# A pipelined Mamba stage kernel: starting each stage's side work 19 units sooner, and loading its inputs part by part

## The chip, the cores and the metric

The kernel runs on one core of one Trainium2 chip. The metric is device time in microseconds (us) for the whole program; lower is better. A core has five engines that matter here, each with its own queue of instructions which it works off in order: TensorE (PE, matrix products, whose weight loads the profile lists as PEld), VectorE (DVE), ScalarE (ACT), GpSimd (POOL) and SyncE (SP), which in this kernel only issues DMA transfers. Sixteen DMA engines move the data of all transfers.

## The reference

Four layers, each `x = x + layer(group_norm(x))`, work on four images of 96 channels and 64 x 64 pixels in float32.

- Layer 0: an attention over super-pixels, with a 5 x 5 depthwise convolution beside it.
- Layer 1 ("l1"): a projection to 192 channels, a 3 x 3 convolution, then a selective scan along four ways through the image (rows forward, rows backward, columns forward, columns backward), whose four outputs are summed, normalised over the channels, gated, and put through a small convolution net.
- Layer 2: a 3 x 3 convolution.
- Layer 3 ("l3"): convolutions, again a selective scan along four ways, the sum, a normalisation, a gate and a channel mixing.

The scan is the heavy part. For 192 channels, 16 states and 4096 steps it computes `h = h * exp(delta * A) + delta * u * B`, then `y = sum over states of h * C`. The sum of the four ways needs the two row ways and, turned by a transpose of the image, the two column ways:

```python
y = oy[:, 0] + inv[:, 0] + why + invwhy
```

Layers 1 and 3 have one scan for each of the four images, so there are eight scans.

## The kernel before

**Stages and units.** The eight scans run one after another in the order of `SCANS` (line 37): l1 of images 0 and 1, l3 of images 0 and 1, l1 of images 2 and 3, l3 of images 2 and 3. Each is a stage, numbered 0 to 7. A stage has 32 groups: four ways, four chunks of 1024 steps, two halves of 96 channels. A group has 12 units of 8 channels x 16 states = 128 rows. So a stage has `per` = 384 units, and the program 3072. What comes ahead of stage 0 (layers 0 and the input of layer 1 of image 0) and behind stage 7 runs alone.

**One unit.** `unit` (line 2160) writes out the instructions of one unit on all engines: SP fetches the decay rows of the unit four ahead (`fetch`, line 2065, 512 KB into one of twelve `rep` buffers; `AHEAD` = 4), ACT makes exponentials of those of the unit two ahead (`decays`, line 2073), DVE scans (`scan`, line 2093) and multiplies with B (line 2086), POOL multiplies with C (line 2105), PE spreads inputs (`drive`) and, each fourth unit, sums over states (`collect`). When a group ends, `output` (line 2125) puts its sum into `yo`, and at the start of the next unit SP stores it to `y_row` or `y_col` in DRAM and counts `stored[0]` up by one. Group g of the program counts as stored in unit 12 (g + 1) + 2.

**Side work.** Beside a stage runs the work of another image that is not the scan: `BESIDE` (line 38) names it. Beside stages 0, 3 and 4 it is `first` (layer 0 and the input of l1 of the next image), beside 1, 2, 5 and 6 `second` (the end of l1 for an image whose scan is done, layer 2 and the input of l3), beside 7 three times `third` (the end of l3 and of the program) and then `last`, which is `third` for the image that is being scanned. These are generators. Each `yield` ends a step and says what it is charged: nothing (None) for a step on PE, charged by its matmul time, a number in half microseconds for others, `WAIT` for the whole rest of the unit.

**The planner.** Each unit gets a budget of `PACE` of its stage, in us of PE time. The unit's own `drive` costs 0.43 of it and `collect`, each fourth unit, 1.71. The class `Slots` then takes steps in up to three places of the unit for as long as 0.3 or more is left; a debt is carried over. So PACE sets how densely the side work is strewn, and where in the stage it ends. In the main loop (line 2256 on) the work of a stage begins at its unit 0. At unit `per - NG - LEAD - 1` = 365 all that is left of it is written out at once (`work.run()`), since at 366 the first group of the next stage is prepared from what it made. From 365 to 383 nothing runs beside the scan.

**The sums' loads.** `second`, `third` begin with `directions` (line 1529). For each half h of the channels it waits until the scan's outputs are stored, then loads the row sum into V and the column sum into a tile `yc`, in chunks of 1024 columns. y_row and y_col hold 96 channels in four blocks of 24 rows with 8 rows of gap behind each, so `ungapped` (line 1118) issues four transfers of 24 rows for each chunk: 32 for each half, all from one slot, then a charge of 4. Then come 16 turns: ACT copies 512 columns of `yc` transposed (line 1546), PE adds the row part and the turned part, ACT copies the sum to V (line 1556). `last` and, for its late chunks, `finish` use `ungapped` too.

**Group norm beside the scan.** `group_norm_on_scalar` (line 1161) has 4 copies with a sum, 8 squares with a sum and 4 scalings on ACT, each charged 1. **Several generators at once.** `weave` (line 1307) goes round among up to `depth` generators, moving on after each step that has a number.

Of the kernel before, what the change touches and what calls it, by code (L numbers as in the profile page):

```python
# [9 lines left out]
F32 = mybir.dt.float32  # L10
# [7 lines left out]
B, C, H, W = 4, 96, 64, 64  # L18
# [9 lines left out]
CH = 1024  # L28
NCH = L // CH
# [7 lines left out]
SCANS = (("l1_", 0), ("l1_", 1), ("l3_", 0), ("l3_", 1), ("l1_", 2), ("l1_", 3), ("l3_", 2), ("l3_", 3))  # L37
# [1 line left out]
          (("first", 3),), (("second", 2),), (("second", 3),), (("third", 0), ("third", 1), ("third", 2), ("last", 3)))  # L39
GN_EPS = 1e-5  # L40
PHI_EPS = 1e-12
PACE = (2.95,3.45,3.45,2.95,2.95,3.45,3.45,3.2)


PHI_SAFE = 10.0
# [154 lines left out]
def _view(t, slot, rows=None):  # L200
    n, m, shape = slot
    v = t[: rows or t.shape[0], n : n + m]
    if len(shape) == 1:
        return v
    names = "abcd"[: len(shape)]
    return v.rearrange(f"p ({' '.join(names)}) -> p {' '.join(names)}",
                       **{k: s for k, s in zip(names, shape)})
# [693 lines left out]
def streams(ctx: ExitStack, tc: tile.TileContext, x, wts, cst, out, wat, cat, flag):  # L901
# [3 lines left out]
    nc = tc.nc  # L905
# [12 lines left out]
    cols = keep.tile([128, 5], F32, name="cols")  # L918
# [88 lines left out]
    def img(t):  # L1007
        return t.rearrange("p (a b) -> p a b", b=W)
# [8 lines left out]
    def mm(o, lhsT, rhs, first=True, last=True):  # L1017

        lhsT, rhs = lhsT[:], rhs[:]
        if lhsT.shape[0] == 96 and lhsT.tensor.name in padded and rhs.tensor.name in padded:  # L1020
            lhsT, rhs = full(lhsT), full(rhs)
        n = 1
        for d in rhs.shape[1:]:
            n *= d
        m = o.shape[0]
        passes = 1 if rhs.dtype == BF16 else 1.07 if m == 32 else 2 if m == R + 2 * N else 4
        spent[0] += n * passes / 2400
        nc.tensor.matmul(o, lhsT=lhsT, rhs=rhs, start=first, stop=last)  # L1028
# [4 lines left out]
    def bank():  # L1033
        if solo[0]:
            if not spare:
                t = ps.tile([128, CH], F32, tag="bx", name="bx")
                spare.extend((t[:, PCH:], t[:, :PCH]))
            return spare.pop()
        return ps.tile([128, PCH], F32, tag="one", name="one")
# [47 lines left out]
    with Stack(1) as T:  # L1087
        t0 = T.tile([128, cst.shape[1] - n2], F32, name="t0")
        nc.scalar.dma_start(out=t0, in_=cst[:, n2:])
        n, m, shape = wat["l1_alog"]  # L1090
# [4 lines left out]
        n, m, shape = cat["spread"]  # L1095
        nc.vector.tensor_copy(spread.rearrange("p a b -> p (a b)"), t0[:, n - n2 : n - n2 + m])
        for tag in ("l1_", "l3_"):
            decay[tag] = keep.tile([128, 4, E // 8], F32, name=tag + "decay")
            n, m, shape = cat[tag + "alogn"]
            src = _view(t0, (n - n2, m, shape))  # L1100
            if tag == "l3_":
                nc.scalar.activation(decay[tag], src, AF.Exp)
                src = decay[tag]
# [7 lines left out]
    def image(name, rows=96):  # L1111
        return [dram.tile([rows, L], F32, name=f"{name}{b}") for b in range(B)]
# [3 lines left out]
    y_row, y_col = ([image(f"{k}{h}_", 128) for h in range(2)] for k in ("yrow", "ycol"))  # L1116

    def ungapped(dst, src, cols):

        for q in range(4):  # L1120
            nc.sync.dma_start(out=dst[24 * q : 24 * q + 24], in_=src[32 * q : 32 * q + 24, cols])

    def group_norm(src, dst):

# [32 lines left out]
    def group_norm_on_scalar(src, dst):  # L1161

        st = small.tile([96, 8], F32, name="gs_st")
        for j in range(4):
            s = src[:, bass.ts(j, CH)]
            nc.scalar.activation(s, s, AF.Copy, accum_out=st[:, j : j + 1])
            yield 1
        mv = small.tile([96, 4], F32, name="gs_mv")
        nc.vector.tensor_reduce(mv[:, 0:1], st[:, 0:4], AX.X, ALU.add)
        yield 0.5  # L1170
        p = bank()
        mm(p[:96, 0:1], group[:96], mv[:, 0:1])
        yield
        nc.scalar.activation(mv[:, 1:2], p[:96, 0:1], AF.Copy, scale=-1.0 / L)
        yield 0.5
        for j in range(8):
            p = bank()
            nc.scalar.activation(p[:96], src[:, bass.ts(j, PCH)], AF.Square, bias=mv[:, 1:2], accum_out=st[:, j : j + 1])
            yield 1
        nc.vector.tensor_reduce(mv[:, 2:3], st, AX.X, ALU.add)  # L1180
        yield 0.5
        p = bank()
        mm(p[:96, 0:1], group[:96], mv[:, 2:3])
        yield
        nc.scalar.activation(mv[:, 2:3], p[:96, 0:1], AF.Sqrt, bias=eps[:96], scale=1.0 / L)
        yield 0.5
        nc.vector.reciprocal(mv[:, 2:3], mv[:, 2:3])
        nc.vector.tensor_mul(mv[:, 3:4], mv[:, 1:2], mv[:, 2:3])
        yield 0.5
        for j in range(4):  # L1190
            nc.scalar.activation(dst[:, 16 * j : 16 * j + 16, :], img(src)[:, 16 * j : 16 * j + 16, :], AF.Identity,
                                 scale=mv[:, 2:3], bias=mv[:, 3:4])
            yield 1

    def diagonals(pool, w, name="diag"):

# [110 lines left out]
    def weave(made, depth):  # L1307

        left, active = list(made), []
        while left or active:  # L1310
            if left and len(active) < depth:
                active.append(left.pop(0))
            for g in list(active):
                while True:
                    try:
                        v = next(g)
                    except StopIteration:
                        active.remove(g)
                        break
                    yield v  # L1320
                    if v is not None and not isinstance(v, tuple):
                        break

    def attention(b, xn, w, samp, dist):
# [204 lines left out]
    def directions(V, b, tag):  # L1529

        with Stack(1) as T:
            full = len(groups) // len(SCANS) * (SCANS.index((tag, b)) + 1)
            cols = []
            for h in range(2):
                while stored[0] < full - 1 + h:
                    yield WAIT
                t = T.tile([96, W, H], F32, name="yc", bufs=2)
                cols.append(t)
                for j in range(4):
                    ungapped(t.rearrange("p a b -> p (a b)")[:, bass.ts(j, CH)], y_col[h][b], bass.ts(j, CH))  # L1540
                    ungapped(V[:, h, bass.ts(j, CH)], y_row[h][b], bass.ts(j, CH))
                yield 4

            def turned(n):
                y = T.tile([96, PCH], F32, name="yt", bufs=2)
                nc.scalar.copy(img(y), cols[n // 8][:, :, 8 * (n % 8) : 8 * (n % 8) + 8].rearrange("p a b -> p b a"))  # L1546
                return y

            y = turned(0)
            for n in range(16):  # L1550
                v = V[:, n // 8, bass.ts(n % 8, PCH)]
                p = bank()
                mm(p[:96], ident[:96, :96], v, True, False)
                mm(p[:96], ident[:96, :96], y, False, True)
                yield
                nc.scalar.copy(v, p[:96])
                if n < 15:
                    y = turned(n + 1)
                yield 1

    def second(b):

# [362 lines left out]
    NG = 96 // 8  # L1925
    WAIT = "wait"
# [134 lines left out]
    def fetch(i):  # L2061

        g, m = place(i)
        rep = sp.tile([128, CH], F32, name="rep", bufs=12)
        nc.sync.dma_start(out=rep, in_=ready[g][1][8 * m : 8 * m + 8, :].unsqueeze(0).to_broadcast([N, 8, CH]))
        live[i] = [rep]
# [76 lines left out]
    AHEAD, BEHIND, LEAD = 4, 2, 6  # L2143
    DRIVE, SUM, SLOT = 0.43, 1.71, 0.5
    total = len(groups) * NG
    per = total // len(SCANS)
    store, waiting, stored, owed = [], [], [0], 0.0
# [5 lines left out]
    def catch_up(n):  # L2153
        for w in waiting:
            w[0] -= n
        for w in [w for w in waiting if w[0] <= 0]:
            waiting.remove(w)
            w[1]()
# [74 lines left out]
    def beside(s):  # L2233
        stages = {"first": first, "second": second, "third": third, "last": last}
        for n, b in BESIDE[s]:
            yield from stages[n](b)
# [3 lines left out]
    with tc.manual_schedule():  # L2240
        for _ in prepare(0):
            catch_up(9)
        catch_up(9)
        prep = Slots(prepare(1))
        for _ in range(LEAD):
            prep.begin(0)
            prep.end()
            catch_up(1)
        for i in range(AHEAD):
            fetch(i)  # L2250
        decays(0)
        decays(1)
        drive(0)
        drive(1)
        times_b(0)
        for i in range(total):
            s, at = divmod(i, per)
            g, m = divmod(i, NG)
            if at == 0:
                work, owed = Slots(beside(s)), 0.0  # L2260
            if m == NG - LEAD and g + 2 < len(groups):
                prep.run()
                prep = Slots(prepare(g + 2))

            if at == per - NG - LEAD - 1 and s < len(SCANS) - 1:
                work.run()

            owed = min(owed, 0.6) + PACE[s]
            owed = unit(i, prep, work, owed)
        for j in range(total - 4, total, 4):  # L2270
            collect(j)
            output(j)()
            stored[0] += 1
# [14 lines left out]
    p = bank()  # L2288
# [37 lines left out]
```

## Time and profile before

| What | us |
|---|---|
| median of 3 runs | 13741.8 |
| lowest and highest | 13741.55, 13748.16 |
| the profiled execution | 13771.14 |
| its span, first to last instruction | 13769.2 |
| ahead of the first scan | 648 |
| stage 0 | 1602 |
| stages 1 to 6, each | 1575 to 1581 |
| stage 7 | 1929 |
| behind the last scan | 122 |

Busy shares of the span: DVE 84%, PE 81% (matmuls are pipelined, so this isn't the share of its peak), POOL 75%, ACT 63%; mean granted clock of TensorE 0.901. The DMA engines were busy 76.2% of their time with SP's transfers.

Stage boundaries are the starts of the 1st, 385th, 769th, ... of the 3072 scan instructions (line 2093). Any unit's start is found in the same way, so a stretch of units of a stage is a stretch of time, and the busy times of all engines in it can be read. In stage 2 the last 19 units, with nothing beside the scan, take 73.1 us, or 3.85 each; the 143 units of side work in which PE has convolutions take 540.0, or 3.78 each.

### The profile page before, as it was taken

The page shows a single profiled execution, that of the slowest core. Times are in us where ns is not written, and L with a number is a line of the kernel's source. Part 1 is how long each engine was busy: PE and PEld are TensorE (multiplying, and loading weights), DVE is VectorE, ACT ScalarE, POOL GpSimd, SP SyncE. Part 2 cuts the span into 40 slices and gives each one's busy share as a digit, 9 for nine tenths or more (in the row PEclk, how much of TensorE's full clock was granted, in tenths as well). Part 3 has the DMA queues.
Part 4 walks back from the last instruction along what each step waited for, and adds up shares of the span by engine and source line. Part 5 has one row for each costly group of instructions (what it writes and reads, how often), then busy time and mean ns, then how long its engine had stood idle before and what let it go on. Part 6 is the DMA issues. An engine that isn't in the chain of part 4 may idle for free. (4 is left out here: it accounts for less than half of the span.)

```text
span 13769.2 us, 128385 instructions
## 1 busy us (share of the span) xinstructions
PE 11150.4 (81%) x40802; PEld 3349.2 (24%) x40802; DVE 11633.7 (84%) x7509; ACT 8718.5 (63%) x12338; POOL 10280.4 (75%) x4730
## 2 busy tenths in 40 slices
PE   9888886988779896888868887898969887777756
PEld 3322221322223221222212221232313222111111
DVE  1488998998889988889988898898889988887886
ACT  3366576667756676665766566667756676665654
POOL 1178887888878877788877888787878878666674
PEclk9899998999889897999989998998979998888867
DMA  0277788787878888778877788797888878777674
GB/s 11 68 172 197 200 224 215 201 218 203 224 195 223 210 210 212 188 194 214 232 190 198 195 216 227 192 228 198 213 214 204 224 201 229 185 196 188 172 195 115
DMA packets 840849, 2682.51 MB, mean 195 GB/s; under 512 B 111264, under 2 KB 113792, under 8 KB 840160
## 3 DMA queue, kind: packets, MB, share of 16 engines
q1 hardware_dynamic: 839504, 2672.34, 76.2%
q8 instruction: 324, 5.31, 0.2%
q14 instruction: 365, 2.99, 0.1%
q10 hardware_dynamic: 656, 1.87, 0.0%
HBM read 2179.90 MB, written 493.88 MB: 194 GB/s over the span
## 5 line engine op out<-in xcount | busy, mean ns | idle before, releaser
L2105 POOL TENSOR_TENSOR rep<-hs,bc 128x1024 f32<-128x1024 f32 x3072 | 7221.1, 2357 | 2404.3 <-DVE hs L2093 2012.5
L1028 PE MATMUL one<-arena 128*96 128x512 f32 (+5 forms) x11072 | 5294.0, 604 | 583.9 <-ACT arena L1394 134.2
L2093 DVE TENSOR_TENSOR_SCAN hs<-rep,carry,bx 128x1024 f32<-128x1024 f32 x2304 | 5400.8, 2344 | 302.1 <-ACT rep L2073 36.2
L2086 DVE TENSOR_TENSOR bx<-bx,bc 128x1024 f32<-128x1024 f32 x3072 | 3717.8, 1210 | 683.6 <-PE bx L1028 677.9
L2073 ACT ACTIVATE rep<-rep,l_decay 128x1024 f32<-128x1024 f32 x3072 | 3496.2, 1143 | 764.1 <-DMA rep<-dd 743.3
L1028 PE MATMUL bx<-parts,spread 128*128 128x512 bf16 x6144 | 2030.3, 415 | 1338.7 <-DVE hs L2093 1225.9
L1028 PEld LDWEIGHTS one<-arena 128*96 128x96 f32 (+4 forms) x11072 | 1793.8, 172 | 3053.6 <-issue 1783.9
L2093 DVE TENSOR_TENSOR_SCAN hs<-rep,bx 128x1024 f32<-128x1024 f32 x768 | 1754.5, 2285 | 138.6 <-ACT carry L2101 57.8
L1028 PE MATMUL acc<-rep,ct 128*32 128x512 f32 x12288 | 1721.9, 674 | 7.0 <-POOL rep L2105 7.0
L1028 PEld LDWEIGHTS <-spread 128*128 128x128 bf16 x6144 | 446.9, 100 | 3663.4 <-DVE hs L2093 2374.3
L1028 PE MATMUL one<-pr,ct 64*96 64x512 f32 x1024 | 628.5, 698 | 76.1 <-ACT pr L1980 27.0
L1394 ACT ACTIVATE arena<-one 128x512 f32<-128x512 f32 x576 | 342.2, 594 | 495.3 <-PE one L1028 493.7
L1028 PEld LDWEIGHTS acc<-rep,ct 128*32 128x32 f32 x12288 | 359.4, 118 | 1169.3 <-issue 944.6
L2073 ACT ACT_TABLE_LOAD x492 | 631.2, 1283 | 8.8
L2101 ACT COPY carry<-hs 128x1 f32<-128x1 f32 x2304 | 408.7, 177 | 219.6 <-DVE hs L2093 216.9
L1028 PE MATMUL bx<-arena 128*96 128x512 f32 (+5 forms) x1120 | 489.2, 575 | 21.3 <-ACT arena L1808 3.2
L1028 PE MATMUL one<-arena,ct 128*96 128x512 f32 x508 | 293.9, 686 | 255.3 <-ACT arena L1546 194.5
L1028 PE MATMUL held<-arena,cols 128*32 128x256 f32 x3072 | 481.2, 395 | 12.3 <-ACT arena L1394 11.5
L1028 PE MATMUL held<-arena 128*32 128x256 f32 x3072 | 481.7, 395 | 0.0
L982 POOL MEMSET arena<- 32x1024 f32 (+5 forms) x81 | 54.0, 690 | 393.6 <-ACT arena L1394 321.5
L2015 ACT ACT_TABLE_LOAD x256 | 328.4, 1283 | 4.4
L1028 PE MATMUL one<-us,wt 128*38 128x512 f32 x1024 | 282.3, 674 | 49.1 <-DMA us<-urow 23.7
(3322 smaller groups left out, 9879.5 us busy)
## 6 DMA issues: line engine op xcount, KB each, us to landing
rep<-dd SPq DMA_DIRECT2D x3072, 512.0 KB
parts<-du SPq DMA_DIRECT2D x1024, 144.0 KB
bc<-rows SPq DMA_DIRECT2D x256, 512.0 KB
dd<-delta SPq DMA_DIRECT2D x256, 384.0 KB
du<-cut SPq DMA_DIRECT2D x256, 384.0 KB
yrow<-yo SPq DMA_DIRECT2D x128, 512.0 KB
ycol<-yo SPq DMA_DIRECT2D x128, 512.0 KB
us<-urow SPq DMA_DIRECT2D x128, 384.0 KB
```

The lines of the kernel that those rows point to most:

```text
L982: nc.gpsimd.memset(arena[96:, k : min(k + CH, a + n)], 0.0)
L1028: nc.tensor.matmul(o, lhsT=lhsT, rhs=rhs, start=first, stop=last)
L1394: nc.scalar.activation(last.rearrange("p a b -> p (a b)"), p, AF.Exp, scale=HD**-0.5)
L2015: nc.scalar.activation(w, w, AF.Ln)
L2073: nc.scalar.activation(a, a, AF.Exp, scale=decay[tag][:, k, NG * h + m : NG * h + m + 1])
L2086: nc.vector.tensor_mul(bx, bx, ready[i // NG][2][:, 0, :])
L2093: nc.vector.tensor_tensor_scan(out=hs, data0=a, data1=bx, initial=carry[:, h, m : m + 1] if c else 0.0, op0=ALU.mult, op1=ALU.add)
L2101: nc.scalar.copy(carry[:, h, m : m + 1], live[i][1][:, CH - 1 : CH])
L2105: nc.gpsimd.tensor_tensor(a, hs, ready[i // NG][2][:, 1, :], ALU.mult)
```

## The change

- The side work of stage s + 1 begins at unit 365 of stage s, as soon as the rest of stage s's is written out, 19 units sooner than before. The pace of the next stage holds from there on. Stage 0's begins as before.
- `ungapped` issues one transfer instead of four: its source is seen as 4 blocks x 24 rows x columns, its destination as 96 rows.
- `directions` issues one part (1024 columns of the row sum or the column sum of a half) and gives the rest of the unit back, in `second`; in `third` two parts a unit. The parts of the way that is scanned last wait for just their own groups to be stored; the chunk that is stored last is loaded last. The second half's parts are issued between the turns of the first half, each of which now ends with a WAIT.
- The steps of the group norm on ACT are charged 3, 2 and 3 instead of 1 each.
- `weave` stays with a generator after a step charged 0.5.
- PACE goes from 3.45 to 3.38 beside stages with `second`, from 2.95 to 2.9 in stages 3 and 4, and from 3.2 to 3.25 in stage 7.

```diff
           (("first", 3),), (("second", 2),), (("second", 3),), (("third", 0), ("third", 1), ("third", 2), ("last", 3)))
 GN_EPS = 1e-5
 PHI_EPS = 1e-12
-PACE = (2.95,3.45,3.45,2.95,2.95,3.45,3.45,3.2)
+PACE = (2.95,3.38,3.38,2.9,2.9,3.38,3.38,3.25)


 PHI_SAFE = 10.0
@@ -1117,12 +1117,8 @@

     def ungapped(dst, src, cols):

-        for q in range(4):
-            nc.sync.dma_start(out=dst[24 * q : 24 * q + 24], in_=src[32 * q : 32 * q + 24, cols])
-
-
-
-
+        nc.sync.dma_start(out=dst,
+                          in_=src.rearrange("(q r) c -> q r c", q=4)[:, :24, cols])

     def group_norm(src, dst):

@@ -1164,7 +1160,7 @@
         for j in range(4):
             s = src[:, bass.ts(j, CH)]
             nc.scalar.activation(s, s, AF.Copy, accum_out=st[:, j : j + 1])
-            yield 1
+            yield 3
         mv = small.tile([96, 4], F32, name="gs_mv")
         nc.vector.tensor_reduce(mv[:, 0:1], st[:, 0:4], AX.X, ALU.add)
         yield 0.5
@@ -1176,7 +1172,7 @@
         for j in range(8):
             p = bank()
             nc.scalar.activation(p[:96], src[:, bass.ts(j, PCH)], AF.Square, bias=mv[:, 1:2], accum_out=st[:, j : j + 1])
-            yield 1
+            yield 2
         nc.vector.tensor_reduce(mv[:, 2:3], st, AX.X, ALU.add)
         yield 0.5
         p = bank()
@@ -1190,7 +1186,7 @@
         for j in range(4):
             nc.scalar.activation(dst[:, 16 * j : 16 * j + 16, :], img(src)[:, 16 * j : 16 * j + 16, :], AF.Identity,
                                  scale=mv[:, 2:3], bias=mv[:, 3:4])
-            yield 1
+            yield 3

     def diagonals(pool, w, name="diag"):

@@ -1318,7 +1314,7 @@
                         active.remove(g)
                         break
                     yield v
-                    if v is not None and not isinstance(v, tuple):
+                    if v is not None and not isinstance(v, tuple) and v != 0.5:
                         break

     def attention(b, xn, w, samp, dist):
@@ -1530,16 +1526,24 @@

         with Stack(1) as T:
             full = len(groups) // len(SCANS) * (SCANS.index((tag, b)) + 1)
-            cols = []
-            for h in range(2):
-                while stored[0] < full - 1 + h:
-                    yield WAIT
-                t = T.tile([96, W, H], F32, name="yc", bufs=2)
-                cols.append(t)
-                for j in range(4):
-                    ungapped(t.rearrange("p a b -> p (a b)")[:, bass.ts(j, CH)], y_col[h][b], bass.ts(j, CH))
-                    ungapped(V[:, h, bass.ts(j, CH)], y_row[h][b], bass.ts(j, CH))
-                yield 4
+            cols = [T.tile([96, W, H], F32, name="yc", bufs=2) for _ in range(2)]
+
+            def fetched(h):
+                col = cols[h].rearrange("p a b -> p (a b)")
+                ways = [(y_row, V[:, h, :]), (y_col, col)]
+                if tag == "l3_":
+                    ways.reverse()
+                for n, (image_, to) in enumerate(ways):
+                    for c in range(NCH):
+                        while stored[0] < (full - 8 + 2 * c + h + 1 if n else full - 8):
+                            yield WAIT
+                        js = bass.ts(NCH - 1 - c, CH)
+                        ungapped(to[:, js], image_[h][b], js)
+                        if tag == "l1_" or c % 2:
+                            yield WAIT
+
+            yield from fetched(0)
+            more = fetched(1)

             def turned(n):
                 y = T.tile([96, PCH], F32, name="yt", bufs=2)
@@ -1554,9 +1558,13 @@
                 mm(p[:96], ident[:96, :96], y, False, True)
                 yield
                 nc.scalar.copy(v, p[:96])
+                if n == 7:
+                    yield from more
                 if n < 15:
                     y = turned(n + 1)
                 yield 1
+                next(more, 0)
+                yield WAIT

     def second(b):

@@ -2256,16 +2264,17 @@
         for i in range(total):
             s, at = divmod(i, per)
             g, m = divmod(i, NG)
-            if at == 0:
-                work, owed = Slots(beside(s)), 0.0
+            if i == 0:
+                work, owed = Slots(beside(0)), 0.0
             if m == NG - LEAD and g + 2 < len(groups):
                 prep.run()
                 prep = Slots(prepare(g + 2))

             if at == per - NG - LEAD - 1 and s < len(SCANS) - 1:
                 work.run()
-
-            owed = min(owed, 0.6) + PACE[s]
+                work, owed = Slots(beside(s + 1)), 0.0
+
+            owed = min(owed, 0.6) + PACE[min(s + (at >= per - NG - LEAD - 1), len(SCANS) - 1)]
             owed = unit(i, prep, work, owed)
         for j in range(total - 4, total, 4):
             collect(j)
```

## The prediction

> **What bounds the kernel now.** First the busy times by stretch. Stage 2 stands for the four stages with `second`; its stretches are units 0-15 (sums' loads and turns), 15-36 (normalisation), 36-179 (convolutions), 179-219 (group norms), 219-287, 287-345 (convolution for l3), 345-365 and 365-384. Columns: stretch, its length, busy time (count) of PE, PEld, DVE, ACT, POOL, then clock, DMA share, GB/s. The next three lines are of stage 3: 0-7 (group norm), 274-282 (the other), 355-384. The last two are of stage 7: units 0-15 and 288-314.
>
> ```profile
> 3827.50:3917.20 89.70, 56.14 (x174) 16.27 (x174) 54.39 (x34) 51.68 (x74) 50.75 (x23) 0.82 0.80 200
> 4026.90:4566.90 540.00, 515.00 (x1729) 169.73 (x1727) 506.26 (x304) 351.73 (x508) 473.01 (x213) 0.98 0.87 215
> 4566.90:4729.70 162.80, 124.89 (x413) 38.22 (x414) 149.59 (x102) 110.21 (x166) 131.90 (x66) 0.84 0.81 204
> 5255.90:5334.20 78.30, 42.11 (x133) 6.90 (x134) 71.79 (x43) 45.00 (x61) 63.97 (x29) 0.59 0.91 244
> 5334.20:5407.30 73.10, 40.80 (x134) 6.65 (x126) 67.26 (x39) 35.50 (x39) 60.21 (x27) 0.66 0.91 223
> ...
> 5407.30:5440.90 33.60, 15.17 (x52) 2.93 (x54) 27.95 (x19) 27.38 (x46) 27.40 (x13) 0.60 0.90 238
> 6556.80:6593.00 36.20, 16.71 (x59) 3.95 (x58) 32.97 (x23) 26.79 (x42) 27.66 (x13) 0.67 0.82 214
> 6874.70:6988.50 113.80, 59.50 (x190) 10.69 (x190) 103.03 (x60) 58.67 (x69) 93.36 (x42) 0.64 0.92 237
> ...
> 11718.40:11801.20 82.80, 53.82 (x166) 15.22 (x166) 52.96 (x32) 49.08 (x71) 49.91 (x23) 0.83 0.84 214
> 13200.20:13296.70 96.50, 56.82 (x180) 9.73 (x180) 92.45 (x56) 57.76 (x83) 84.24 (x38) 0.62 0.88 224
> ```
>
> See three things. In the convolutions PE (515 of 540) and DVE (506) are both full, 3.78 us a unit. In units 345-384 PE falls to half: the planner was through with the side work at 345 of 365 (stage 3: at 355), and a unit still takes 3.9, because the scan alone fills DVE (139 of 151). So 39 units run with PE idle. And units 0-15 take 89.7, 5.98 each, with no engine full. 3.71 each in the last line (26 units that wait for outputs) is my base of a bare unit, so this start loses 89.7 - 15 x 3.7 = 34.
>
> Why it does: first SP's issues in order of time (start, length, instruction), then the waits of 3827-3900 (who waits, for whom, us in total, times, longest).
>
> ```profile
> 3821.82 0.52 SPq L2065 DMA_DIRECT2D rep<-dd  x1
> ...
> 3823.95 2.54 SPq L1121 DMA_DIRECT2D arena<-ycol  x4
> ...
> 3842.82 1.16 SPq L2065 DMA_DIRECT2D rep<-dd  x2
> ...
> 3867.78 0.52 SPq L2065 DMA_DIRECT2D rep<-dd  x1
> ```
> ```profile
> PEld one L1028 <- ACT arena L1546: 35.9, 11, 14.6
> ACT rep L2073 <- DMA rep<-dd: 15.3, 2, 14.4
> ACT arena L1546 <- DMA arena<-ycol: 10.9, 1, 10.9
> ```
>
> Twice 32 loads stand in SP's queue between two fetches: 21 us from 3821.8 to 3842.8, then 23 up to 3867.8, where a fetch is issued four units ahead, some 15 us. So a decay waits for its rows up to 14.4 us, the turned copy (L1546) for its column sum 10.9, and PE behind it 35.9.
>
> Two more lines tell what one DMA engine needs: the page's queue, and a microsecond of quiet near the start of the program.
>
> ```profile
> q1 hardware_dynamic: 839504, 2672.34, 76.2%
> ...
> q1 hardware_dynamic: 62, 0.25, 64.5%
> ```
>
> Mean: 0.762 x 16 x 13769 us / 2672.34 MB = 0.257 us per 4096 B. Quiet: 0.645 x 16 / 62 = 0.166 us for a packet of 4096 B.
>
> **What the skill says.** "DMA: Bandwidth & Descriptors", "Why a DMA increments its semaphore by 16 and not by 1": a transfer runs on k engines, the largest k up to 16 that divides the slowest dimension of both its sides, and they are the lowest-numbered ones; its "Rules for kernel authors" add that an outermost dimension below 16 confines a transfer to so many engines. The old 24 rows give 12; in the burst the DMA share was 0.70 to 0.8, which fits. The new source has 4 blocks outermost: **four engines**, 24 rows each. No transfer of the kernel before has that shape. "TensorE: Matmul & The Clock Gate", "Part 1: The HAM clock gate": idle PE halves its clock; here 0.59-0.66 in the bare units, 0.98 in convolutions, so I charge denser work with no loss of clock.
>
> **The change, part by part.** The planner is arithmetic, so what it will do can be counted. In `second` a part goes out a unit from 365 on, the eighth waits for its group, stored at 374, and then come about three turns in four units: a turn is charged 1.71, its WAIT takes the rest of a unit, and a unit with `collect` has room for the turn alone, whose WAIT then takes the next. So the first stretch grows from 15 units to 35, from 365 to unit 15 of the next stage. The other work had 329 units x 2.59 (3.45 less 0.43 and a quarter of 1.71), 852 in all; with 2 x 12 more for two group norms (16 ACT steps that cost 8 now cost 20), at 2.52 a unit, it needs about 347. Counted slot by slot it ends at 360: nothing is left to be written out in a lump at 365, with 5 units to spare. Per `second`, in us, bare units at 3.7:
>
> - Loads and turns, transfers aside: 35 x 3.7 = 129.5.
> - The transfers' stall. A part puts 24 packets on each of four engines; ordinary traffic is 223 GB/s x 3.85 / 16 = 13 packets a unit and engine. With p us a packet, 16 parts in 22 units load these four with 16 x 24p + 22 x 13p against 22 x 3.7 = 81.4. I take p = 0.18: above the quiet 0.166, as the other twelve engines then idle part of the time; ends 0.141 (96 KB at the skill's 27 GiB/s per engine, "Specifications") and 0.257. That is 69 + 51.5 - 81 = 39; fetches four ahead for decays two ahead cover two units, 8; the turned copy behind the last part, stored in the same unit, adds 4: 35. Together 164.5 against 89.7: **+75**. The SP time of 64 issues goes.
> - Normalisation 0. Convolutions +6 units less 6, as PE's share falls by 2%: +16. Group norms +5 units less half of the 15 that 40 units lose over 3.7, since ACT's bursts are spread: +11. 219-287 +1 unit less 3: +1. 287-345 +2 units less 2: +5.
> - The `weave` edit: in 8 steps a stage DVE's multiplication is issued right behind ACT's tanh that it waits for, and frees its bank sooner. Nothing in the trace prices it; 1 us each, 8 a stage, either way, and I take 0.
> - Bare units: 39 become 5: -34 x 3.88 = **-132**.
>
> Sum -23.5, times four: **-94**. Stages 3 and 4 (373 units instead of 354; no sums' loads): group norms +6 units less 3 and +5 less 4, other steps +7 less 2, bare -18 x 3.92: -13 each, -27. Stage 0 hands 19 units on: +8 units for its norms less 8 us, -27 bare units x 3.88: **-83**.
>
> Stage 7 takes them: three runs of loads and turns (units 0-15, 93-108, 185-198), 43 units in 82.8 + 85.2 + 82.7 = 250.7, become 77, two parts a unit. Here 16 parts go out in 10 units: 69 + 23.4 - 37 = 55.5, less 8, plus 5: 52 each. 77 x 3.7 + 156 = 441, **+190**; other steps -5 units, -18; `last`, whose 8 parts go out in two slots, 4 x 4.3 us each on four engines where 16 transfers took 7 of SP, +10; its wait for outputs 26 units to 16, -37. Together +145. The 122 behind the end, tied to the last output, stays.
>
> Total -94 - 27 - 83 + 145 = -59: the profiled execution's 13771.1 becomes 13712; the median of the runs lay 29 below the profiled one, so **13683**.
>
> **Rivals.**
>
> - Slower: the four engines are the new bound. Place: units 365 to 3 of each `second`, ten units of each `third`. Per 0.01 in p a `second` loses 6.7 and a `third` 5.1, 42 in all. At 0.194 the gain is gone, at 0.23 it is 13893, at 0.257 14006. For it: the mean is 0.257, and SP waits in order for landings (du, rows) that would stand in the same four queues. Against it: much of that mean is sixteen engines at once. Decides at p = 0.20.
> - All sixteen engines carry it after all: then only bytes count, some 3.9 a unit in 35 and 77 units; `second` -51 each, stage 7 -15: 13411. Against it: the rule above and 0.70 in the burst.
> - The gap isn't worth it: bare units at 3.9 are hardly longer than full ones at 3.78, so moving work into them gives only what it thins out. With half of the thinning lost (about 50 of 99 in the sums above), 13733: no change. A lump at 365 would need the slots to be miscounted by more than 5 units; 2.5 us of PE for each beyond.
>
> **How the numbers follow.** From no change this kernel's measurement tells about 0.2%, 27 us. Four engines with p below 0.187: 0.48, 13557 (p = 0.15) to 13715, with the forecast 13683 in it; p to 0.20 or a smaller gain from the gap: 0.12; p above: 0.33; sixteen engines: 0.07. Faster 0.55, same 0.12, slower 0.33. The range leaves out sixteen engines and p above 0.23: 13520 (p = 0.141) to 13900.
>
> **What would show it.** Right: SP has no gap between fetches above some 10 us at stage starts; PE stays full up to 360; the last 19 units show a DMA share well below 0.91 while ACT waits for rep or ycol transfers; stage 7's first run takes above 100 us for some 25 units. Wrong: a DMA share near 0.95 there (sixteen engines), a burst of PE work at 365 (lump), DVE waits on the tanh above 8 a stage (`weave`), or convolutions as long as before.

## The result, and the profile after

The changed kernel took 13854.9 us (median of four runs, 13851.0 to 13859.5) beside 13741.7 for the kernel before (13733.4 to 13748.2): a ratio of 1.0080, with a 95% interval of 1.0067 to 1.0092. It is 113 us slower: inside the range of the prediction, but the forecast was a gain of 59.

The profiled execution's span went from 13769.2 to 13854.5, with the mean clock as before (0.904 and 0.901). Since work was moved across the stage boundaries, I compare stages from 19 units ahead of their start to 19 units ahead of the next; on this basis the 73 us of bare units that stage 0 hands to stage 7 appear in neither. Stage times are of one profiled execution of each kernel; stages whose code is the same in two kernels differed by up to 10 us, so I lean on differences that come back in several stages.

| stretch of units | predicted, us | measured, us |
|---|---|---|
| stages 1, 2, 5, 6 (`second`) | -23.5 each, -94 | +22.0, +29.6, +17.5, +31.4: +100.5 |
| stages 3, 4 (`first`) | -13 each, -27 | -27.5, -35.3 |
| stage 0 | -10 | -38.2 |
| stage 7 | +72 | +91.4 |
| ahead of the first scan, behind the last | 0 | -5.8 |
| sum | -59 | +85 |

The sign was lost in the four `second`. The page's queue line and the decays' group, of after, come first (group: busy us, mean ns | idle us and what ended most of it):

```profile
q1 hardware_dynamic: 833520, 2672.32, 75.1%
...
L2081 ACT ACTIVATE rep<-rep,l_decay 128x1024 f32<-128x1024 f32 x3072 | 3502.8, 1144 | 1097.1 <-DMA rep<-dd 1078.6
```

The bytes are the same 2672.3 MB, but exponentials now wait 1079 us in all for their decay rows (743 before). Busy times by stretch of after, in the prediction's columns: stage 2, units -19 to 16 (the new loads and turns), 37 to 186 (convolutions), 360 to 365 (all that is left without side work); then stage 7, units -19 to 7, 83 to 109, 182 to 208 (the three runs of loads and turns of `third`):

```profile
3735.00:3931.60 196.60, 98.43 (x302) 25.95 (x302) 123.74 (x73) 93.05 (x119) 112.69 (x50) 0.69 0.71 186
4051.10:4615.10 564.00, 521.72 (x1746) 172.61 (x1776) 529.85 (x320) 361.19 (x517) 496.12 (x223) 0.97 0.86 217
5324.50:5343.60 19.10, 8.42 (x30) 1.43 (x34) 18.50 (x12) 14.78 (x15) 17.85 (x9) 0.63 0.87 261
...
11641.10:11796.00 154.90, 76.03 (x243) 20.76 (x242) 92.62 (x55) 74.06 (x91) 86.25 (x38) 0.75 0.68 187
12168.30:12320.40 152.10, 72.43 (x221) 19.61 (x224) 90.33 (x52) 72.48 (x93) 84.94 (x41) 0.71 0.63 176
12699.30:12847.90 148.60, 77.40 (x224) 20.80 (x229) 91.90 (x55) 71.60 (x96) 90.33 (x44) 0.71 0.68 189
```

The planner did what was counted: side work ends at 360, and the bare units left are five. But 35 units of loads and turns take 196.6 us, where 35 bare units at 3.7 are 129.5, and the DMA share there (0.71, last but one column) is *lower* than in the bare units before (0.91): something waits for DMA while DMA isn't full. Who waits, in the stretch 3735.0 to 3931.6 of after:

```profile
ACT rep L2081 <- DMA rep<-dd: 50.0, 13, 11.1
PEld one L1028 <- ACT arena L1550: 44.5, 9, 25.5
PE one L1028 <- ACT arena L1550: 37.0, 5, 23.8
```

and in the same units of the kernel before (3755.1 to 3922.0), their length and the decays' wait:

```profile
3755.10:3922.00 166.90, 99.83 (x316) 23.79 (x308) 126.14 (x77) 94.71 (x122) 115.82 (x51) 0.76 0.85 213
...
ACT rep L2073 <- DMA rep<-dd: 22.6, 8, 14.4
```

The decays' rows are late by 50.0 us in all, where they were late by 22.6, and the turned copy (L1550) still holds up PE. That points at the transfers, but not yet at why.

### The profile page after: what moved, and what is told of

Its sections match the earlier page's. It is cut to its first block, busy times and chain, and to the rows that moved or that the text cites. A ratio compares the mean times of both kernels' runs of the same rounds, so it can differ in the third digit from the quotient of the medians.

```text
span 13854.5 us, 126995 instructions
## 1 busy us (share of the span) xinstructions
PE 10972.8 (79%) x40141; PEld 3349.9 (24%) x40802; DVE 11618.7 (84%) x7509; ACT 8713.1 (63%) x12332; POOL 10279.4 (74%) x4730
## 5 line engine op out<-in xcount | busy, mean ns | idle before, releaser
L1028 PE MATMUL one<-arena 128*96 128x512 f32 (+4 forms) x11072 | 5281.0, 603 | 626.6 <-ACT arena L1390 143.4
L1028 PE MATMUL bx<-parts,spread 128*128 128x512 bf16 x5483 | 1854.9, 413 | 1362.0 <-DVE hs L2101 1179.8
L1028 PEld LDWEIGHTS one<-arena 128*96 128x96 f32 (+3 forms) x11072 | 1798.5, 172 | 3024.9 <-issue 1863.6
L1028 PE MATMUL acc<-rep,ct 128*32 128x512 f32 x12288 | 1662.2, 654 | 21.9 <-POOL rep L2113 18.8
L1028 PE MATMUL one<-arena,ct 128*96 128x512 f32 x508 | 323.1, 749 | 312.5 <-ACT arena L1550 186.0
```

## The experiments

The kernel before took 13741.7 to 13762.8 us as the median of the different sets of runs, so I compare ratios to it (with 95% intervals in brackets), and turn a difference of ratios into us with 13750.

### How many DMA engines carry a part

Theory A: the single transfer runs on four engines, and its 24 packets on each of them cost the time. Theory B: it is the rest of the change, the parts' order and place and the denser side work. The first kernel undoes one edit of after, the shape of the transfer:

```diff
-        nc.sync.dma_start(out=dst,
-                          in_=src.rearrange("(q r) c -> q r c", q=4)[:, :24, cols])
+        for q in range(4):
+            nc.sync.dma_start(out=dst[24 * q : 24 * q + 24], in_=src[32 * q : 32 * q + 24, cols])
```

> The change with only its first edit undone: each part is four transfers of 24 rows again, still issued part by part from 19 units sooner. Theory A (one transfer with 4 blocks outermost runs on four of the sixteen DMA engines, and their queue is what stalls): the runs of loads and turns lose their stall, 58 us each in four and 52 in three, and last some 20; 13450, from 13350 to 13560. Theory B (the engines don't matter; the stall is the order: a part behind the store it waits for, the turns' waits): the stalls stay, SP gets 48 more issues of 0.4 us a run; 13855 to 13980.

Measured: 13595.4 us, ratio 0.9886 (0.9868 to 0.9905), 260 us better than after and 35 above theory A's range. The second keeps one transfer, but with 96 rows outermost; for that it reads 96 rows in a run, gaps included, so partly the wrong ones.

```diff
-        nc.sync.dma_start(out=dst,
-                          in_=src.rearrange("(q r) c -> q r c", q=4)[:, :24, cols])
+        nc.sync.dma_start(out=dst, in_=src[0:96, cols])
```

> The change with each part read as one transfer of the first 96 rows of the image in place of four blocks of 24 (so the sums are made of partly wrong rows; sizes and count of transfers are the change's). Outermost dimension 96 instead of 4. Theory A: as the four transfers or a little better, 13430, from 13330 to 13540. Theory B: 13855 within 30.

Measured: 13541.5, ratio 0.9852 (0.9835 to 0.9868), just above theory A's range. The third goes the other way: two transfers a part, each of two blocks.

```diff
-        nc.sync.dma_start(out=dst,
-                          in_=src.rearrange("(q r) c -> q r c", q=4)[:, :24, cols])
+        for p in range(2):
+            nc.sync.dma_start(out=dst[48 * p : 48 * p + 48],
+                              in_=src.rearrange("(q r) c -> q r c", q=4)[2 * p : 2 * p + 2, :24, cols])
```

> The change with each part in two transfers whose outermost dimension is 2. Theory A: two engines with 48 packets each a part: 16 x 24 more packets at 0.2 us on the two, +75 us in each of seven runs: 14380, from 14200 to 14600. Theory B: 16 more issues of 0.65 us a run, hidden: 13855 to 13900.

Measured: 14327.4, ratio 1.0419 (1.0398 to 1.0440). The fourth puts the single transfer alone into the kernel before.

> The kernel before with only the one transfer a part, still all from one slot at the stage's unit 0. Theory A: each burst of 8 parts is 8 x 24 packets at 0.2 us, 38 us on four engines, where 32 issues took 17 of SP: +40 in each of seven runs, +10 in last: 14030, from 13930 to 14130. Theory B: SP's 64 issues of 0.4 us a run go and the decays come in time: -20 to -30 a run, 13560.

Measured: 14006.8, ratio 1.0186 (1.0165 to 1.0206).

A stands, though the first two kernels gained a little less than it said: something else is left of the stall (next section). B falls. The same stretch, stage 2 units -19 to 16, with 96 rows outermost:

```profile
3696.80:3849.60 152.80, 89.45 (x302) 23.17 (x303) 123.01 (x73) 92.65 (x119) 112.84 (x50) 0.80 0.94 239
```

and with two blocks outermost:

```profile
3788.90:4042.50 253.60, 95.67 (x302) 24.79 (x303) 123.72 (x72) 92.37 (x118) 112.73 (x50) 0.67 0.54 142
```

The instructions of the five engines are nearly the same in number and length. The DMA share falls from 0.94 over 0.71 to 0.54, and the time rises from 153 over 197 to 254. The number of transfers does not order the times: one a part with 96 rows outermost (13541), one with four blocks (13855), two with two blocks (14327), four with 24 rows (13595). The outermost dimension does. The kernel with 96 rows also reads other rows, but the one with 24 rows reads the right ones and is close to it.

How many engines work can be counted, too. The traces hold the start and the length of each packet, and so how many packets are under way at each moment. In these 35 units of stage 2 exactly four are under way for 47 us in after, and for 1 us or less with 24 or 96 rows outermost; exactly two for 106 us with two blocks, and for 4 us or less in the others; exactly twelve for 20 us with 24 rows, and for 6 or less in the other three. Over the whole program exactly four are under way for 460 us in after and for 79 with 96 rows. This agrees with the rule that the prediction took from the Trainium skill's "DMA: Bandwidth & Descriptors", "Why a DMA increments its semaphore by 16 and not by 1": a transfer runs on the largest number of engines, up to 16, that divides the slowest dimension of both its sides. The runs add the price: this stretch takes 44 us more with four blocks outermost than with 96 rows, and 101 more with two blocks.

### What the other stall is

With 96 rows outermost 153 - 129.5 = 23 us are left, and 30 with transfers of 24 rows, where I had expected little. Two suspects: SP's queue, or the bytes. First SP. SP's issues in stage 2 of after (start, length):

```profile
3791.68 1.08 SPq L2149 DMA_DIRECT2D ycol<-yo  x1
3809.57 0.66 SPq L1120 DMA_DIRECT2D arena<-ycol  x1
3810.34 0.53 SPq L2073 DMA_DIRECT2D rep<-dd  x1
```

For 17 us SP issues nothing between the store of a group and the load of the part just stored, and a fetch waits behind it. SP's own waits in 3735.0 to 3931.6 name what it waits for:

```profile
SPq L1120 <- DMA ycol<-yo: 23.9, 2, 15.2
```

So in after the load of that part was put off by two units:

```diff
+                        if tag == "l1_" and n and c == NCH - 1:
+                            yield WAIT
+                            yield WAIT
                         js = bass.ts(NCH - 1 - c, CH)
```

> The kernel after with one edit: in `second` the part that was stored last is loaded two units after its store instead of in the same unit, twice a stage. Theory S (SP stands on the landing of the store, some 17 us in stage 2 of after, while fetches wait behind it in its queue, and this is the part of the stall that the four engines do not explain): units -10 to -4 lose most of that wait, 8 to 15 us for each `second`, so about 13810 (13795 to 13825). Theory Q (the four engines' backlog sets the end whatever SP does): 13855, within 10; slower than 13865 if the two units that the turns come later are not hidden.

Measured: 13841.2, ratio 1.0053 (1.0036 to 1.0070). That is 14 us less than after by the medians and 37 by the ratios, with runs from 13823 to 13860: the time alone doesn't tell S from Q, and lies between the two. The trace tells more. SP's wait for the store, in units -19 to 16 of stage 2 of this kernel, fell from 23.9 to:

```profile
SPq L1120 <- DMA ycol<-yo: 9.9, 2, 9.4
```

and its units -19 to 0 and 0 to 16 took:

```profile
3740.40:3852.60 112.20, 44.74 (x147) 9.96 (x143) 67.39 (x40) 40.86 (x46) 60.74 (x27) 0.67 0.73 185
3852.60:3936.10 83.50, 48.53 (x153) 13.55 (x154) 56.12 (x33) 51.92 (x72) 50.98 (x23) 0.80 0.72 185
```

In after these were 123.8 and 72.8: what was won ahead of the boundary was given back behind it, 195.7 against 196.6. The four stages with `second` take 0 to 7 us less each than in after, where S wants 8 to 15. So S falls: this wait of SP is worth a few us of a stall of 67 at most, and is mostly a place where the backlog shows.

Then the bytes: four transfers reduced to two, half of the rows.

```diff
-        for q in range(4):
+        for q in range(2):
```

> The kernel after with the sums' loads as transfers of 24 rows again (13595.4 with all four), but only two of the four blocks are loaded, so half the bytes; the other 48 rows of the sums hold what lay there, and the result is not the reference's. Theory Y (the stall that is left beside the four engines, about 26 in a `second` and 21 to 30 in a `third`, is the time of the bytes, 16 parts of 393 KB at 215 to 240 GB/s being 26 to 29 us, since the scan's own traffic fills the DMA engines): half of it goes, some 12 for each of four `second` and three `third` and 5 of `last`, about 13505 (13480 to 13530). Theory T (it is the turns on ACT and PE, or the order in SP's queue): 13570 to 13600.

Measured: 13486.9, ratio 0.9806 (0.9786 to 0.9826), 110 us below the kernel with all four. Units -19 to 16 of stage 2, with all rows and then with half:

```profile
3701.60:3861.30 159.70, 93.04 (x301) 24.43 (x302) 123.51 (x72) 93.05 (x120) 112.69 (x50) 0.75 0.90 229
```
```profile
3683.50:3828.00 144.50, 89.45 (x302) 22.91 (x302) 123.25 (x73) 91.78 (x117) 112.56 (x50) 0.81 0.91 228
```

This is theory Y. Half the loads, half the stall: 30 becomes 15, with every turn still made and nearly the same throughput, 228 GB/s; as means, 31 becomes 14 in the four `second` and 26 becomes 14 in the three `third`. A `second` loads 16 parts of 393 KB, 6.3 MB, and at 229 GB/s these are 27 us. Half the rows are also half the issues of SP, but those aren't it: with 96 rows outermost SP issues still fewer, 16 transfers a `second` instead of 32, with all the bytes, and the mean stall is 24. DMA was at 0.91 in the bare units before, which leaves these bytes little room to hide there.

All five doses in one row, by the packets of a part on the engine with the most of them, a part being 96 packets of 4096 B, spread over 16, 12, 4 and 2 engines (and half of them over 12):

| packets of a part on the busiest engine | ratio | us for each further packet |
|---|---|---|
| 4 (half the bytes, 12 engines) | 0.9806 | |
| 6 (96 rows, 16 engines) | 0.9852 | 0.25 |
| 8 (24 rows, 12 engines) | 0.9886 | 0.18 |
| 24 (four blocks, 4 engines) | 1.0080 | 0.13 |
| 48 (two blocks, 2 engines) | 1.0419 | 0.15 |

The last column divides each step over the 128 parts of the program (8 scans x 16). The two large steps are known within 0.02, the two small ones only within 0.14 by their intervals. So from 8 packets on a further one costs most of its whole time, 0.166 in quiet, and little of it is hidden. Nor did spreading help: alone in the kernel before, in bursts, the single transfer costs 0.0186; in the changed kernel, one part a unit, 1.0080 - 0.9886 = 0.0194.

### What the rest of the change is worth

The rest gained 0.0114 with transfers of 24 rows, 157 us. These kernels take it apart. The earlier start is undone first: transfers of 24 rows, PACE of before, and

```diff
-            if i == 0:
-                work, owed = Slots(beside(0)), 0.0
+            if at == 0:
+                work, owed = Slots(beside(s)), 0.0
...
-                work, owed = Slots(beside(s + 1)), 0.0
```

> The kernel after with four transfers of 24 rows again in `ungapped` (13595.4 in an earlier run), and in it each stage's side work begun at its unit 0 again, with the PACE of before; the part-by-part loads, the charges and the weave edit stay. Theory G (filling the 19 bare units is worth what the prediction's sums give it, bare units at 3.85 against 2.6 to 3.8 for a unit that takes over work): the stages with `second` go back to about their time before (13 each lost), stages 3 and 4 lose some 15 each, stage 7 some 15, so about 13690 (13650 to 13730). Theory N (a bare unit is hardly longer than a full one, so the start does not matter, and the gain of 13595 comes from the parts and charges): 13580 to 13620. In the trace, bare units from 365 to 383 come back under both, 72 us a stage.

Measured: 13587.4, ratio 0.9870 (0.9854 to 0.9887), beside 0.9886 with the earlier start: theory N, in the total. In stage 2 units 56 to 186 of this kernel, convolutions at PACE 3.45, are

```profile
4055.30:4537.60 482.30, 470.84 (x1575) 159.81 (x1601) 457.94 (x268) 311.13 (x443) 423.18 (x185) 1.00 0.89 224
```

or 3.71 a unit. With the earlier start, at PACE 3.38, units 56 to 179 take 456.7, also 3.71. PE is busy for 440.7 us of these, and for 445.2 of the same 123 units at 3.45: the lower PACE took 1% of PE's work out, and the units did not get shorter.

Next the charges: the three `yield`s of the group norm at 1 again, in the kernel with transfers of 24 rows.

> The kernel after with four transfers of 24 rows again in `ungapped` (13595.4), and in it the group norm's steps on ACT charged 1 each again. Theory C (spreading ACT's bursts is worth the units that it takes: group norms of a `second` took 157 to 163 us in 40 units before and 171 to 176 in 45 after, 2.6 us for each unit more, where a bare unit costs 3.85): the side work of a `second` ends some 9 units sooner, so about 12 more for each of four, 5 for each of stages 3 and 4, about 13655 (13630 to 13680). Theory D (the charges move units about and no more): 13580 to 13615.

Measured: 13653.9, ratio 0.9918 (0.9902 to 0.9935): the charges are worth 44 us (58 between the medians), theory C's total. But C had it from the `second` and stages 3 and 4; stage 0 alone gives 37, 1528.8 instead of 1492.1, and the `second` give 7, 12, 10 and 8. Then the edit of `weave` alone, in the kernel before:

```diff
-                    if v is not None and not isinstance(v, tuple):
+                    if v is not None and not isinstance(v, tuple) and v != 0.5:
```

> The kernel before with the edit of `weave` alone (it stays with a generator after a step charged 0.5). The prediction put 0 on it, with 8 us a stage with `second` either way as the ends. Theory W0: 13740, within 15. Theory W+ (DVE is held up behind the tanh): 32 or more slower, 13772 and up. Theory W- (banks come free sooner): 13710 and below.

Measured: 13705.9, ratio 0.9956 (0.9939 to 0.9972), 60 us: theory W-. It was gained where its steps are: units 287 to 345 of stage 2 took 245.0 before, and with the edit

```profile
4988.60:5225.00 236.40, 215.90 (x696) 71.48 (x708) 206.25 (x122) 192.38 (x251) 194.84 (x90) 0.97 0.85 224
```

with DVE's multiplications waiting less for PE there:

```profile
DVE bx L2086 <- PE bx L1028: 12.9, 7, 6.3
```

(20.9 us in 11 waits before.) That fits banks that come free sooner; no run separates it from other effects of the new order. Two more kernels add to this edit the part-by-part loads alone, in transfers of 24 rows, and the charges alone. Taking the edit of `weave` out of the changed kernel wasn't tried.

> The kernel before with the edit of `weave` (0.9956 of before, alone) and with the part-by-part `directions` of after, its loads as four transfers of 24 rows; PACE, start and charges of before. Theory P (the parts take SP's two queues of 32 loads apart: the stall of a `second` over bare units of 3.7 falls from 34 to 26 as in the late-start run, so 8 to 15 each for four, stage 7 some 10): 13640 to 13680, a ratio of 0.991 to 0.995. Theory Z (bytes set this stall, so the order of the loads does nothing): as the edit of `weave` alone, 13690 to 13720.

Measured: 13722.8, ratio 0.9976 (0.9967 to 0.9985), 3 us above theory Z. P falls; with `weave` alone it was 0.9956, so the parts gain nothing and may lose a little. Stages 1, 5 and 7 take 4, 3 and 16 us less than with `weave` alone, stages 2 and 6 22 and 16 more. This kernel also gives the earlier start its other half: from 0.9976 here to 0.9918 in the kernel with the charges undone (its PACE differs too) are 80 us, and 75 of them lie in stages 3 and 4 (1589.6 and 1578.7 against 1550.8 and 1542.9). So the earlier start is worth something in places: in `first` it gives what the charges give, and once they are there, little more.

> The kernel before with the edit of `weave` and the group norm's charges of after (3, 2, 3); loads, PACE and start of before. Theory C (spreading ACT's bursts is worth what undoing it cost, 44 to 58, most of it in stage 0, where the late end of the side work takes the place of idle units): 13640 to 13670, a ratio of 0.991 to 0.993. Theory D (it was worth something only together with the part-by-part loads): 13690 to 13720.

Measured: 13668.8, ratio 0.9941 (0.9922 to 0.9961), between the two: stage 0 gains 33 and stages 3 and 4 33 and 17, and the `second` lose 8 to 11 each. Parts and charges together, the late-start kernel, reach 0.9870, more than the sum of the two. That the charges help `second` only with the parts shows in all four stages; why stays open.

The last kernel gives the earlier start back to stages 3 and 4 alone.

> The late-start kernel (four transfers of 24 rows, part-by-part loads, charges and weave of after, start and PACE of before; 13587.4, 0.9870 of before) with the 19 units' earlier start and PACE 2.9 given back to stages 3 and 4 alone. Theory F (the earlier start pays where the side work's own chain sets the unit, as in `first`, and not in `second`, whose units of convolution take 3.7 whatever the PACE): stages 3 and 4 take some 1548 each instead of 1561 and 1552, no other stage changes, about 17 less in all, a ratio of 0.9850 to 0.9865. Theory N (it pays nowhere): 0.9870 and above, stages 3 and 4 at 1552 to 1561.

Measured: 13567.9, ratio 0.9862 (0.9846 to 0.9879). Stage 4 took 10 us less than in the late-start kernel, stage 3 took 3 more, and stage 0, whose code is the same, 10 less: the ratio is where F put it, but the stages do not show F, and the three kernels with transfers of 24 rows at 0.9862, 0.9870 and 0.9886 can't be told apart. They beat both kernels of the case, the one before by 1.1 to 1.4%.

## Why the prediction was wrong

The forecast of -59 us can be split in two: -330 for the change if sixteen engines carry the loads (its second rival, 13411), and +272 for four engines at p = 0.18. The runs answer each part. The change with 96 rows outermost gained 0.0148, 203 us (236 between the profiled spans), 127 less than the first part. Four engines in place of sixteen cost 1.0080 - 0.9852 = 0.0228, 313 us, 41 more than the second. So about three quarters of the miss have nothing to do with the four engines.

**The four engines** were right in kind and nearly in size. 272 became 313, which on the forecast's scale (42 us per 0.01) is p = 0.19, still below the break-even of 0.194. So the slower rival had the right mechanism but not the deciding size: at p = 0.19 the forecast would have been "no change".

**The step that failed** is "loads and turns", 32 us too low in each `second`, with "convolutions +6 units less 6" (9 too low) and "normalisation 0" (7) behind it; four times these are 190 of the 194 us by which the four `second` missed. A `second`, mean of the four, by the prediction's own sums:

| units after | predicted | after | 96 rows outermost |
|---|---|---|---|
| -19 to 16, loads and turns | 164.5 | 196.1 | 153.9 |
| 16 to 37, normalisation | 112.7 | 119.7 | 119.2 |
| 37 to 186, convolutions | 556 | 564.9 | 564.7 |
| 186 to 231, group norms | 172 | 173.7 | 174.0 |
| 231 to 360 | 529 | 528.6 | 525.6 |
| 360 to 365 | 19.4 | 19.2 | 18.9 |

- Loads and turns: the stall was put at 35 and was 67, of which 42 go with the four engines (196.1 - 153.9) and 24 stay without them. I had taken a load for free once the busiest engine had room for it, and charged sixteen engines 3.9 a unit, 7 us. That room wasn't there. At p = 0.18 the 13 packets of ordinary traffic keep an engine busy for 2.3 us of a unit of 3.7, a share of 0.63, while my own line for bare units showed DMA at 0.91. So the 6.3 MB had to be paid, 24 us, and halving them halved the stall.
- Convolutions: the 6 us for 2% less PE work weren't there, and 3 more were lost. PE and DVE both looked full (515 and 506 of 540), and taking PE work out did not shorten the unit; what sets its 3.7 us was not found. With it goes the worth of filling bare units in `second`: with the charges in place, the earlier start gained nothing there (the four took 3 to 9 us longer with it), as the third rival said.
- Normalisation was put at 0 and took 7 more in after, 5 to 7 with any transfer. No run here explains it.

**What was right.** Each `third` was put at a stall of 52 and measured 58.7, 55.9 and 52.4 (154.9 less 26 x 3.7, and so on); but by luck, since 120, 116 and 110 us with 96 rows outermost make it 37 of engines and 19 of bytes, where I had only engines. The counts of the planner, the bare units' price, the group norms and the stretch from 231 on held within 3 us. So did three of the signs named: PE's work up to 360, a DMA share well below 0.91 in the last 19 units (0.68, beside waits for rows), stage 7's first run above 100 (154.9). The fourth, no gap between fetches above 10 us, did not: SP stood 17. And a sign of error showed: convolutions 3.79 a unit, 3.77 before.

**Sizes missed on the good side.** `weave` was put at 0, with 8 a stage either way as its ends; alone it gained 60 us, 9 to 14 for each `second`. Of its two mechanisms the gain fits the banks that come free sooner; the ends were too tight. Stage 0 gained 38 where I had 10, and giving the charges back takes 37 of it: I had put 8 us on what thinner ACT bursts give back. Stages 3 and 4 gained 63 instead of 27; charges alone give 50 there, the start alone 75, and neither adds much to the other.

## What to carry to other kernels

Before transfers are merged, look at the outermost dimension of both sides and count the packets on the engine that gets most of them: here, from 8 packets a part to 48, each further one cost the end 0.13 to 0.15 us, in a burst as well as one part a unit. Where the DMA share is at 0.9, expect a load to cost the time of its bytes; sending it part by part instead of in a burst gained nothing here. Check a sum for the engines' time against the share that the trace shows before the load is added. And before a thinner budget is credited with time, find a stretch with a different budget and see whether its units are any shorter.

## What was not expected of the hardware

- One transfer in place of four saved SP's time as meant (0.66 us against 1.53 us for four in the kernel with 24 rows, at 3759.7), and lost far more in flight: SP's time was not what was short.
- DMA engines held up the kernel at a mean share of 0.54 to 0.71, with exactly two or four packets under way for 106 and 47 us of the stretch; the mean over sixteen hides it, and a count of the packets under way shows it.
- A packet's price at the end of the program was nearly the same from 8 to 24 packets and from 24 to 48 (0.13 and 0.15 us each): no dose in this range was free.
